# A graph network layer on one core: three-operation features on ScalarE, an earlier last adjacency load, earlier statistics

## The chip, the cores and the metric

The kernel runs on one core of a Trainium2 chip. The metric is device time in microseconds (us) of one execution; before the change the median of 3 runs was 1814.86 us (1811.27 to 1817.74).

A core has several engines, each with a queue of its own that it works through in order. TensorE (PE in the profile) multiplies matrices and writes to PSUM, which has eight banks here; PEld is its loading of weights. VectorE (DVE), ScalarE (ACT) and GpSimd (POOL) do elementwise work. SyncE (SP) only starts transfers (DMAs); ACT and POOL start some too. All DMAs of the core run on the same 16 DMA engines. Semaphores order the engines among each other.

## The reference

There are 32 graphs of 512 nodes with 256 features (x), each with a 512 x 512 adjacency of zeros and ones (adj). Cut to what matters:

```python
h = jnp.maximum(_layernorm(x, axis=-1), 0.0)
# _L0_gnn_ref(h, adj, ...), where h is called x:
xc = jnp.transpose(x, (0, 2, 1))
h = jax.nn.relu(_bn(_conv1d(xc, conv1_w, 0), ...))
h = _bn(_conv1d(h, conv2_w, 8), ...)                       # 17 taps
x_conv = jnp.transpose(jax.nn.relu(h + xc), (0, 2, 1))
s = x @ w_se.T + b_se                                      # 3 values a node
sq = jnp.sum(s * s, axis=-1)
dist = sq[:, :, None] + sq[:, None, :] - 2.0 * jnp.einsum('bnd,bmd->bnm', s, s)
A = jnp.exp(-dist) * mask                                  # mask = adj
msg = jax.nn.relu(x @ w_msg.T + b_msg)
x_nmp = jnp.einsum('bnm,bmd->bnd', A, msg)
x_in = jnp.concatenate([x_conv, x_nmp], axis=-1)
gi, gh = x_in @ w_ih.T + b_ih, x @ w_hh.T + b_hh           # gates r, z, n of a GRU
...
# out = x + (1 - z) * n + z * h
```

## The kernel before

The 32 graphs are worked in two groups of 16 (g = 0, 1), and each group in two stages, a first part and a nodes stage. A last stage makes the gates of all graphs, two graphs (a pair) at a time. All matrices are float32; a matmul appears in the profile as two halves. Within each stage the order of the instructions on every engine is the order of the program's text (`manual_schedule`), so where a line stands decides what it queues behind.

**First part** (`first_part`). For each graph b: `load_x` brings x; `statistics` takes mean and variance on VectorE (bn_stats, bn_aggr, an addition) and the inverse root on POOL (rstd); `normalise` writes xn on VectorE, or for one graph of the second group on ScalarE with a small shift from VectorE ahead of it; `transpose_h` transposes it on TensorE (phT) and clips it on VectorE into hT, which is also stored to DRAM (hd); `conv1` multiplies by w1 (pc), VectorE adds the shift (h) and ScalarE clips; `windows_to_freq` transforms windows of h into 80 frequency rows (px, into xf). In group 0 the 17-tap weights go through the same transform between these steps (pw, wst, stored as wd), and the steps of `load_weights` come one per graph.

**Nodes stage** (`nodes`). Two kinds of work are woven together. One is the convolution in frequency: 40 units a group, each a `product` of three matmuls in place of four (py), for which `prepare` forms two sums on POOL, wsum (128x512) and both (128x256); `load_unit` brings a unit's weights (wt) into one of three buffers. Its result y is stored (yd) through the list `stores`, which `flush` empties in order on SP. The other is the graph product, for the graphs in the order of `todo`. `message` multiplies by wmsg, whose last three columns are w_se: TensorE makes pm, VectorE adds the bias to msg and to the three embedding columns st, ScalarE clips msg. `features` builds from st and its square the factors fl and fr, whose product over 9 rows is the exponent -dist. `factors` transposes them on TensorE (psl, psr), `exponents` multiplies them (pd) and ScalarE takes exp into A. `turn` transposes the adjacency on VectorE, `masked` multiplies A by it. `aggregate7` forms A times msg in seven products, for which `block_sums` makes eight sums on POOL (ms, ts and two in place); the last graphs of group 1 use the plain `aggregate` (L528). `save_nmp` stores the result (nd).

The loop over i takes graph todo[i] and looks ahead: adjacency loads run two graphs ahead, into two buffers by turns, h loads four ahead, message and features two ahead, factors one ahead. At the head of an iteration stand

```python
flush()
...
if len(more) > 1:
    load_adj(more[1], i % 2)
if len(more) > 3:
    load_h(more[3])
```

`more` holds the next four graphs, so it has two left at i = 13, where the last adjacency is loaded. An adjacency is four DMAs of 256 KB. In group 1 the units end at i = 12.

In group 0 the last four units (36 to 39) are left over and are worked in the first part of group 1, in five pieces that `fill()` takes one after the other from the list `left`.

**Gate stage**. `load_pair` and `load_combined` bring the first pair's h (hp), frequencies (yt), nmp (np) and the combined weights (sw) on POOL's queue; `sums` forms POOL sums of them; `inverse` transforms back (L659, pc); the gates multiply by sw in seven products (pg, pn, pz; L671).

Of the kernel before, what the change touches and what calls it, by code (L numbers as in the profile page):

```python
# [13 lines left out]
ALU = mybir.AluOpType  # L14
# [51 lines left out]
def gnn_layer(  # L66
# [131 lines left out]
    def shift_w1():  # L198
# [3 lines left out]
    wmsg = early.tile([P, DC, D + NS], FP, name="wmsg")  # L202
    bmsg = early.tile([P, D + NS], FP, name="bmsg")

    load_weights = [
        partial(nc.sync.dma_start, back, nc.inline_tensor(back_np, name="dft_back").ap()),
        partial(load_rows, wmsg[:, :, :D], w_msgT, nc.sync),
# [2 lines left out]
        partial(nc.sync.dma_start, bmsg[:, D:], b_se.rearrange("t o -> o t").to_broadcast([P, NS])),  # L210
        load_vectors,
        vectors,
    ]


# [2 lines left out]
    fr = early.tile([P, NC, 4, 32], FP, name="fr")  # L218
    nc.vector.memset(fl, 0.0)
    nc.vector.memset(fr, 0.0)  # L220
    nc.vector.memset(fl[:, :, 2 * NS : 3 * NS], 1.0)
    nc.vector.memset(fr[:, :, :, NS : 2 * NS], -1.0)


    WD = dram.tile([ROWS, D * D + 4 * D], FP, name="wd")
# [79 lines left out]
    def transpose_h(b):  # L305
        HT[b] = work.tile([P, DC, N], FP, tag="hT", name=f"hT_{b}")
        for dc in range(DC):
            p = bank(f"phT_{b}_{dc}")
            for c in range(NC):
                nc.tensor.transpose(p[:, c * P : (c + 1) * P], XN[b][:, c, dc * P : (dc + 1) * P], ident)  # L310
            if b == 0 and dc > 0:
                nc.scalar.activation(HT[b][:, dc, :], p, AF.Relu)
            else:
                nc.vector.tensor_scalar(HT[b][:, dc, :], p, 0.0, None, op0=ALU.max)  # L314
        nc.sync.dma_start(HD[b], HT[b])
        del XN[b]
# [136 lines left out]
    def features(b):  # L453

        st = ST.pop(b)
        nc.vector.tensor_mul(st[:, 1], st[:, 0], st[:, 0])
        s1, s2 = (st[:, k, :, None, :].to_broadcast([P, NC, 4, NS]) for k in range(2))
        nc.vector.tensor_copy(fl[:, :, :NS], st[:, 0])
        nc.vector.tensor_copy(fl[:, :, NS : 2 * NS], st[:, 1])
        nc.vector.tensor_scalar(fr[:, :, :, :NS], s1, 2.0, None, op0=ALU.mult)  # L460
        nc.vector.tensor_scalar(fr[:, :, :, 2 * NS : 3 * NS], s2, -1.0, None, op0=ALU.mult)

    def factors(b):

# [421 lines left out]
    def first_part(g, freq, between, left=()):  # L886


        b0, b1 = g * GB, (g + 1) * GB
        for b in range(b0, b0 + 3):  # L890
            if b not in X and (g == 0 or b == b0):
                load_x(b)
        if g == 0:
            t = XN[b0] = pools["first"].tile([P, NC, D], FP, tag="xn", name="rows", bufs=2)
            ones, diags = t[:, 0, :P], t[:, 1:3, :].rearrange("p i (c m) -> p i c m", m=P)
            nc.vector.memset(ones, 1.0)

            for _ in range(5):
                nc.tensor.matmul(row1[1][:, : 2 * P], ident, fr.rearrange("p c g k -> p (c g k)")[:, : 2 * P], start=True, stop=True)
            batch_norm("bn1", scale1, shift1, nc.gpsimd)  # L900
            bn1_row(0, scale1, ones, diags)
            bn1_row(1, shift1, ones, diags)
        if b0 not in STATS:
            statistics(b0)
        normalise(b0)
        if g == 0:
            scale_w1()
            shift_w1()
        left = list(left)

        def fill():
            for step in left.pop(0) if left else ():
                step()

        if g > 0:
            place_h1(b0)
            load_x(b0 + 1)
            fill()
            load_x(b0 + 2)
        transpose_h(b0)  # L920
        fill()
        statistics(b0 + 1)
        normalise(b0 + 1, g > 0)
        fill()
        if g > 0:
            statistics(b0 + 2)
        for b in range(b0, b1):
            if b + 3 < b1:
                load_x(b + 3, nc.sync if b < 3 else nc.gpsimd)
            if b == b0:  # L930
                conv1(b)
                one, two = between(0) if g == 0 else ([], [])
                for step in one:
                    step()
                fill()
                if g == 0:
                    transpose_h(b + 1)
                    statistics(b + 2)
                    normalise(b + 2)
                else:  # L940
                    normalise(b + 2)
                    transpose_h(b + 1)
                fill()
                xf, last_two = freq(g), two
                continue
            if g == 0:

                slots = last_two if b == b0 + 1 else between(b - b0)

                def slot():  # L950
                    for step in slots.pop(0) if slots else ():
                        step()

                if b == b0 + 1:
                    between(b - b0)
                    conv1(b)
                    slot()
                if b == b0 + 2:
                    slot()
                if b == b1 - 1:  # L960
                    by_chunks(b - 1)
                    load_h(b0)
                if b + 2 < b1:
                    statistics(b + 2)
                if b + 1 < b1:
                    transpose_h(b + 1)
                if b > b0 + 2:
                    slot()
                if b + 2 < b1:
                    normalise(b + 2)  # L970
                if b > b0 + 1:
                    conv1(b)
                    slot()
                if b == b1 - 1:
                    by_chunks(b)
                windows_to_freq(b - 1, xf)
                slot()
                continue
            if b == b1 - 1:
                by_chunks(b - 1)  # L980
                load_h(b0)
            if b + 2 < b1:
                statistics(b + 2)
            if b + 1 < b1:
                transpose_h(b + 1)
            if b + 2 < b1:
                normalise(b + 2)
            one, two = between(b - b0)
            conv1(b)
            for step in one:  # L990
                step()
            windows_to_freq(b - 1, xf)
            for step in two:
                step()
        if g > 0:
            by_chunks(b1 - 1)
        windows_to_freq(b1 - 1, xf)
        return xf
# [8 lines left out]
    with tc.tile_pool(name="freq", bufs=1) as fpool:  # L1007
# [33 lines left out]
        def nodes(g, xf, units, last, following=()):  # L1041
# [45 lines left out]
            for i, b in enumerate(todo):  # L1087
                mine = spread(units, i, last) if i < last else []
                more = todo[i + 1 : i + 5]
                seven = i <= last  # L1090

                def bring():
                    if len(more) > 1:
                        message(more[1])
                        features(more[1])

                flush()
                if g + 1 < NG and i == GB // 2:
                    load_x(b1)
                if g + 1 < NG and i == 3 * GB // 4:  # L1100
                    statistics(b1)
                if len(more) > 1:
                    load_adj(more[1], i % 2)
                if len(more) > 3:
                    load_h(more[3])
                if more:
                    factors(more[0])
                if i == 0:
                    bring()
                for u in mine[:1]:  # L1110
                    multiply(u)
                if i > 0:
                    bring()
                if not seven:
                    aggregate(b, [0])
                if more:
                    turn(more[0], [0, 1])
                    exponents(more[0])
                    masked(more[0], [0, 1])
                for u in mine[1:2]:  # L1120
                    multiply(u)
                if more:
                    turn(more[0], [2, 3])
                    masked(more[0], [2, 3])
                if seven:
                    aggregate7(b)
                else:
                    aggregate(b, [1])
                if len(more) > 2:
                    by_chunks(more[2])  # L1130
                stores.append(partial(save_nmp, b))
                for u in mine[2:]:
                    multiply(u)
                if more and i + 1 <= last:
                    block_sums(more[0])
            flush()

        with phase("pw", "ahead"):
# [3 lines left out]
            with phase("first", "sums"):  # L1142
                combine = combine_weights()

                def between(b):

                    if b == GB - 3:
# [4 lines left out]


                pw, (u0, u1, u2, u3) = pools["pw"], range(UNITS - LEFT, UNITS)
                left = [[partial(load_unit, 0, u2, pools["sums"])],
                        [partial(prepare, pw, 0, u1, xf), partial(product, pw, 0, u0, xf), partial(prepare, pw, 0, u2, xf)],
                        [partial(product, pw, 0, u1, xf), partial(load_unit, 0, u3)],
                        [partial(prepare, pw, 0, u3, xf), partial(product, pw, 0, u2, xf)],
                        [partial(product, pw, 0, u3, xf)]]
# [82 lines left out]
```

## Time and profile before

| what | us |
|---|---|
| median of 3 runs | 1814.86 (1811.27 to 1817.74) |
| the profiled execution | 1818.6 |
| its span, first to last instruction | 1816.8 |
| TensorE, VectorE, POOL, ScalarE busy | 1791.6, 1244.6, 779.4, 623.5 |
| first part, nodes of group 0 | to about 157, to about 434 |
| first part, nodes of group 1 | to about 555, to about 851 |
| gate stage | from about 851 |
| one graph in nodes of group 0, of group 1 | 16.5, 19.1 |
| one pair in the gate stage | 59.7 |

Stage ends are where TensorE turns to the next kind of work in the timeline; the periods are the distances of equal steps of neighbouring graphs there. TensorE's granted clock is 0.996 on the mean of the span.

A timeline line gives the start in us from the span's start, the duration, the engine, the source line, the operation, output and inputs, their shapes, and how many neighbours were merged; in brackets stands the idle time just before it and who ended that. SPq, ACTq and POOLq are DMA issues of these queues. A wait line reads: who waited, for whom, us in total, times, longest. A windows line gives for one stretch the length and then the busy us of TensorE, its weight loads, VectorE, ScalarE and POOL, each with its number of instructions, then the granted clock as a share of full speed, the DMA engines' mean busy share and GB/s. "Landing" is the time from a DMA's issue to its completion.

### The profile page before, as it was taken

To read this page: it belongs to the slowest core of one execution; us is meant where nothing else is said; L and a number is where in the kernel's file an instruction comes from. 1 tells how busy PE (TensorE), PEld (TensorE's weight loads), DVE (VectorE), ACT (ScalarE), POOL (GpSimd) and SP (SyncE) were. 2 spreads that over 40 slices of the span, in tenths; PEclk is the share of its full clock that TensorE was granted. 3 is DMA by queue.
4 is the path that set the end of the run, shared out by engine and by line. 5 is a ranking of instruction groups with operands and counts; after the bars stand their busy time and mean duration, and the time that the engine had idled before them with its cause. 6 is when DMAs were issued, how large, how long until landed. Compare 5 with 4: busy or idle time off the path is not lost.

```text
span 1816.8 us, 21203 instructions
## 1 busy us (share of the span) xinstructions
PE 1791.6 (99%) x6974; PEld 1151.6 (63%) x6974; DVE 1244.6 (69%) x2370; ACT 623.5 (34%) x1252; POOL 779.4 (43%) x731
## 2 busy tenths in 40 slices
PE   9999999999999999998999999999999999999998
PEld 6677788887998888884544554455545554555443
DVE  7886988996996778783266546664666456655666
ACT  4556444443345444443212222122212221222121
POOL 3432877777334777775322232213231322133221
PEclk9999999999999999999999999999999999999999
DMA  9999889785769878979142144224432343234412
GB/s 261 305 296 226 239 231 231 220 222 191 251 222 222 243 216 221 253 188 309 23 122 87 35 122 122 87 36 121 122 98 45 101 122 110 52 82 122 118 21 53
DMA packets 307089, 288.27 MB, mean 159 GB/s; under 512 B 146764, under 2 KB 237420, under 8 KB 306596
## 3 DMA queue, kind: packets, MB, share of 16 engines
q1 hardware_dynamic: 296948, 261.44, 53.3%
q0 software_dynamic: 6592, 23.50, 4.2%
q10 hardware_dynamic: 3440, 1.97, 0.4%
q8 instruction: 56, 0.92, 0.2%
q14 instruction: 53, 0.43, 0.1%
HBM read 190.45 MB, written 96.40 MB: 158 GB/s over the span
## 4 chain that ended last, share of the span: by engine, by line
PE 90%; DMA 3%; DVE 3%; issue 2%; POOL 1%; SPq 0%; ACT 0%; ACTq 0%; DVEq 0%; POOLq 0%
PE pg L671 30%; PE pn L671 15%; PE py L394 11%; PE pn L545 9%; PE pm L445 6%; PE pc L330 5%; PE pc L659 5%; PE px L345 3%; PE pd L489 2%; PE pw L254 2%; PE phT L310 1%; DMA adj<-in_adj_dram 1%; DMA wt<-wd 1%; PE pz L671 1%; DMA x<-in_x_dram 1%
## 5 line engine op out<-in xcount | busy, mean ns | idle before, releaser
L649 POOL TENSOR_TENSOR hp<-hp 128x512 f32<-128x512 f32 x64 | 80.4, 1267 | 415.9 <-DMA hp<-hd 325.7
L671 PE MATMUL pg<-hp,sw 128*128 128x512 f32 x434 | 221.8, 593 | 0.7 <-DVE rz L690 0.5
L671 PE MATMUL pg<-np,sw 128*128 128x512 f32 x434 | 221.6, 592 | 0.0
L671 PE MATMUL pg<-cp,sw 128*128 128x512 f32 x434 | 221.6, 592 | 0.0
L649 POOL TENSOR_TENSOR cp<-cp 128x512 f32<-128x512 f32 x64 | 80.5, 1268 | 235.6 <-ACT cp L665 234.3
L361 POOL TENSOR_TENSOR wsum<-wt 128x512 f32<-128x512 f32 x78 | 105.6, 1354 | 121.7 <-DMA wt<-wd 76.9
L686 ACT ACTIVATE rz<-rz,brz 128x512 f32<-128x512 f32 x93 | 67.0, 721 | 260.2 <-DVE rz L690 260.2
L394 PE MATMUL py<-wt,xf 128*128 128x256 f32 x640 | 154.3, 384 | 0.0
L671 PEld LDWEIGHTS pg<-hp,sw 128*128 128x128 f32 x434 | 82.2, 190 | 104.7 <-issue 98.1
L671 PEld LDWEIGHTS pg<-cp,sw 128*128 128x128 f32 x434 | 82.5, 190 | 103.8 <-issue 103.8
L671 PEld LDWEIGHTS pg<-np,sw 128*128 128x128 f32 x434 | 82.5, 190 | 103.8 <-issue 103.8
L394 PEld LDWEIGHTS py<-wt,xf 128*128 128x128 f32 x640 | 117.1, 190 | 35.0 <-issue 19.7
L810 ACT ACTIVATE nt<-nt,vech 128x512 f32<-128x512 f32 x64 | 46.2, 722 | 236.2 <-DVE nt L809 236.2
L330 PE MATMUL pc<-w,hT 128*128 128x256 f32 x512 | 118.3, 384 | 0.8 <-DVE hT L314 0.8
L445 PE MATMUL pm<-wmsg,hq 128*128 128x259 f32 x512 | 117.8, 382 | 0.3 <-DVE nmp L563 0.3
L671 PE MATMUL pn<-np,sw 128*128 128x512 f32 x224 | 114.4, 592 | 0.0
L671 PE MATMUL pn<-cp,sw 128*128 128x512 f32 x224 | 114.4, 592 | 0.0
L671 PE MATMUL pn<-hp,sw 128*128 128x512 f32 x224 | 114.4, 592 | 0.0
L495 DVE TENSOR_TENSOR A<-A,at 128x512 f32<-128x512 f32 x128 | 111.2, 906 | 0.0
L330 PEld LDWEIGHTS pc<-w,hT 128*128 128x128 f32 x512 | 95.4, 191 | 23.8 <-issue 5.6
L445 PEld LDWEIGHTS pm<-wmsg,hq 128*128 128x128 f32 x512 | 96.4, 189 | 15.6 <-DVE nmp L563 0.7
L659 PEld LDWEIGHTS pc<-back,yt 128*128 128x128 f32 x640 | 92.7, 190 | 7.7 <-issue 7.7
(173 smaller groups left out, 3429.2 us busy)
## 6 DMA issues: line engine op xcount, KB each, us to landing
wt<-wd SPq DMA_DIRECT2D x80, 512.0 KB, 7.6
adj<-in_adj_dram SPq DMA_DIRECT2D x128, 256.0 KB, 6.6
wd<-wst SPq DMA_DIRECT2D x64, 320.0 KB, 5.9
yd<-y SPq DMA_DIRECT2D x76, 256.0 KB, 5.1
yt<-yd SPq DMA_DIRECT2D x30, 640.0 KB, 6.8
hd<-hT SPq DMA_DIRECT2D x32, 512.0 KB, 4.6
nd<-nmp SPq DMA_DIRECT2D x32, 512.0 KB, 3.0
xb<-in_x_dram SPq DMA_DIRECT2D x128, 128.0 KB, 3.7
```

Of the source, the lines that this page charges most:

```text
L330: nc.tensor.matmul(p[:, j, :], HT[b][:, ic, c * P : (c + 1) * P], w1[:, ic, :], start=(ic == 0), stop=(ic == DC - 1))
L345: nc.tensor.matmul(p[:, j * 2 * L : (j + 1) * 2 * L], H1[b][:, c0 + j, ic * P : (ic + 1) * P], fwd, start=True, stop=True)
L361: nc.gpsimd.tensor_tensor(t, WT[g, u][:, 0], WT[g, u][:, 1], op=ALU.add)
L394: nc.tensor.matmul(dst, v[:, ic, :], w[:, ic, :], start=(ic == 0), stop=(ic == DC - 1))
L445: nc.tensor.matmul(p[:, : D + NS], hq[:, ic, c * P : (c + 1) * P], wmsg[:, ic, :], start=(ic == 0), stop=(ic == DC - 1))
L495: nc.vector.tensor_mul(A[b][:, mc, :], A[b][:, mc, :], AT.pop((b, mc)))
L545: nc.tensor.matmul(bk, left[:, k, :], right[:, k, :], start=(first and k == 0), stop=(k == 1), skip_group_check=True)
L649: nc.gpsimd.tensor_tensor(t[:, dst, :], t[:, a, :], t[:, b, :], op=sub)
L659: nc.tensor.matmul(bk[:, t0:t1], YT[p][j][:, c, oc * P : (oc + 1) * P], back[:, n : n + t1 - t0], start=(c == 0), stop=(c == len(spans) - ...
L671: nc.tensor.matmul(bk[:, t], sw[:, k, q, o, :], terms[k][q][:, t], start=(first and i == 0), stop=(i == len(ks) - 1), skip_group_check=True)
L686: nc.scalar.activation(rz[:, g, j, :], src, AF.Sigmoid, bias=brz[:, g : g + 1], scale=1.0)
L810: nc.scalar.activation(n, n, AF.Tanh, bias=b_in[:, i : i + 1], scale=1.0)
```

## The change

It has four parts.

1. `features` no longer scales. The embedding's weights and bias are multiplied once by the root of two, on POOL, by a new last step of `load_weights` (`scale_embedding`), and the constants in fl and fr become -0.5, so that the same exponent results from unscaled copies of st and its square. In place of four VectorE operations there are three copies on ScalarE: one for both parts of fl, and one for each of two parts of fr. The square stays on VectorE.
2. In `nodes` the last adjacency (two graphs left) is loaded ahead of `flush()`; the other loads of an iteration stand in a new function `ahead`. For i > 0 it is called where they stood.
3. For i = 0 `ahead` is called after the first unit's `multiply`, which issues the next unit's weight load, so that this goes ahead of one adjacency and one h load.
4. In the first part of group 1 `statistics` of the second and third graph move ahead of a `fill()` each, and the first left-over `prepare` moves from the second piece of `left` to the first. With the left-over work in these places, the second graph's statistics stand ahead of product 36's sums, and the third graph's ahead of product 37's. For group 0 there is nothing in `left`, so this part changes nothing there.

On TensorE the instructions and their order stay the same. On VectorE, apart from the four features operations of each graph, only the order at the start of group 1's first part changes. On POOL two operations are added, and one rstd changes place with the wsum and both of unit 38. On SP nothing is added: in each nodes stage one weight load changes place with an adjacency and an h load, and the last adjacency passes a y store and an nd store in group 0, and one y store in group 1.

```diff
+    def scale_embedding():
+
+        for t in (wmsg[:, :, D:], bmsg[:, D:]):
+            nc.gpsimd.tensor_scalar(t, t, float(np.sqrt(2.0)), None, op0=ALU.mult)
+
     load_weights = [
...
         vectors,
+        scale_embedding,
     ]
...
-    nc.vector.memset(fl[:, :, 2 * NS : 3 * NS], 1.0)
-    nc.vector.memset(fr[:, :, :, NS : 2 * NS], -1.0)
+    nc.vector.memset(fl[:, :, 2 * NS : 3 * NS], -0.5)
+    nc.vector.memset(fr[:, :, :, NS : 2 * NS], -0.5)
...
         nc.vector.tensor_mul(st[:, 1], st[:, 0], st[:, 0])
-        s1, s2 = (st[:, k, :, None, :].to_broadcast([P, NC, 4, NS]) for k in range(2))
-        nc.vector.tensor_copy(fl[:, :, :NS], st[:, 0])
-        nc.vector.tensor_copy(fl[:, :, NS : 2 * NS], st[:, 1])
-        nc.vector.tensor_scalar(fr[:, :, :, :NS], s1, 2.0, None, op0=ALU.mult)
-        nc.vector.tensor_scalar(fr[:, :, :, 2 * NS : 3 * NS], s2, -1.0, None, op0=ALU.mult)
+        nc.scalar.copy(fl[:, :, : 2 * NS].rearrange("p c (k n) -> p k c n", n=NS), st)
+        for k, at in enumerate((0, 2 * NS)):
+            nc.scalar.copy(fr[:, :, :, at : at + NS], st[:, k, :, None, :].to_broadcast([P, NC, 4, NS]))
...
         transpose_h(b0)
+        statistics(b0 + 1)
         fill()
-        statistics(b0 + 1)
         normalise(b0 + 1, g > 0)
-        fill()
         if g > 0:
             statistics(b0 + 2)
+        fill()
...
+                def ahead():
+                    if len(more) > 2:
+                        load_adj(more[1], i % 2)
+                    if len(more) > 3:
+                        load_h(more[3])
+
+                if len(more) == 2:
+                    load_adj(more[1], i % 2)
                 flush()
...
-                if len(more) > 1:
-                    load_adj(more[1], i % 2)
-                if len(more) > 3:
-                    load_h(more[3])
+                if i > 0:
+                    ahead()
                 if more:
                     factors(more[0])
                 if i == 0:
                     bring()
                 for u in mine[:1]:
                     multiply(u)
+                if i == 0:
+                    ahead()
...
-                left = [[partial(load_unit, 0, u2, pools["sums"])],
-                        [partial(prepare, pw, 0, u1, xf), partial(product, pw, 0, u0, xf), partial(prepare, pw, 0, u2, xf)],
+                left = [[partial(load_unit, 0, u2, pools["sums"]), partial(prepare, pw, 0, u1, xf)],
+                        [partial(product, pw, 0, u0, xf), partial(prepare, pw, 0, u2, xf)],
```

## The prediction

> **What bounds the kernel now.** I read the busy table first, then the list of what TensorE waited for, then the timelines around the three longest of those waits.
>
> ```profile
> PE 1791.6 (99%) x6974; PEld 1151.6 (63%) x6974; DVE 1244.6 (69%) x2370; ACT 623.5 (34%) x1252; POOL 779.4 (43%) x731
> ```
>
> TensorE is busy 99% of the span, and the changed program issues the same matmuls in the same order. Faster helpers alone are therefore worth nothing; a change can only win where TensorE stands still. The list of its waits (total us, times, longest) names those places:
>
> ```profile
> PE pn L528 <- DVE A L495: 7.0, 1, 7.0
> PE py L394 <- POOL both L374: 4.0, 1, 4.0
> ...
> PE pn L545 <- POOL ts L520: 1.1, 1, 1.1
> ```
>
> *First place, end of the second nodes stage.* Timelines of SP, VectorE and TensorE, then two slices of the windows view (its last columns: granted clock, DMA share, GB/s):
>
> ```profile
> 815.21 0.32 SPq L568 DMA_DIRECT2D nd<-nmp  x1
> 815.84 1.00 SPq L1057 DMA_DIRECT2D yd<-y  x2
> 816.89 2.68 SPq L414 DMA_DIRECT2D adj<-in_adj_dram  x4
> ```
>
> ```profile
> 838.96 1.30 DVE L478 STREAM_TRANSPOSE at<-adj 128x512 f32<-128x512 f32 x2 [12.48 <-DMA adj<-in_adj_dram]
> ```
>
> ```profile
> 841.74 9.71 PE L528 MATMUL pn<-A,msg 128*128 128x512 f32 x16 [7.04 <-DVE A L495]
> 851.29 5.81 PE L659 MATMUL pc<-back,yt 128*128 128x136 f32 x40
> ```
>
> ```profile
> 812.00:814.00 2.00, 2.00 (x11) 1.77 (x10) 1.97 (x2) 0.41 (x2) 1.92 (x2) 1.00 0.00 0
> 844.00:846.00 2.00, 2.00 (x3) 0.50 (x2) 1.75 (x3) 0.00 (x0) 0.49 (x1) 0.50 1.02 417
> ```
>
> The last graph's adjacency is issued at 816.9, behind two stores, and lands 19.8 us after its last piece was issued, because POOL's first loads of the gate stage start at 818.2 and share the DMA engines. VectorE waits for it until 839, TensorE until 841.7, and then runs at clock 0.50. At 812 to 814 the DMA engines had been idle.
>
> *Second place, start of the second first part.* Timelines of TensorE and POOL:
>
> ```profile
> 453.46 1.21 PE L394 MATMUL py<-wsum,both 128*128 128x256 f32 x4 [3.98 <-POOL both L374]
> 454.46 1.91 PE L310 MATMUL phT<-ident,xn 128*128 128x128 f32 x8
> 456.16 4.43 PE L330 MATMUL pc<-w,hT 128*128 128x256 f32 x16
> ```
>
> ```profile
> 449.64 1.01 POOL L289 TENSOR_TENSOR rstd<-rstd,minus_half 128x4 f32<-128x4 f32 x1 [5.50 <-DVE rstd L288]
> 450.60 0.83 POOL L118 DMA_DIRECT2D x<-in_x_dram  x1
> 451.45 1.28 POOL L361 TENSOR_TENSOR wsum<-wt 128x512 f32<-128x512 f32 x1
> 452.67 0.74 POOL L374 TENSOR_TENSOR both<-xf 128x256 f32<-128x256 f32 x1
> ```
>
> POOL is idle 5.5 us in front of an rstd whose statistics are late on VectorE; the last left-over product's two sums stand behind it and reach TensorE 4 us late.
>
> *Features on VectorE*, in the timeline just ahead of the first place:
>
> ```profile
> 800.71 0.77 DVE L458 COPY fl<-st 128x12 f32<-128x12 f32 x1
> 801.39 1.32 DVE L459 COPY fl<-st 128x12 f32<-128x12 f32 x1
> 802.62 1.32 DVE L460 TENSOR_SCALAR fr<-st 128x48 f32<-128x48 f32 x1
> 803.87 0.78 DVE L461 TENSOR_SCALAR fr<-st 128x48 f32<-128x48 f32 x1
> ```
>
> Four copies of 12 to 48 elements hold VectorE for 3.8 us here; the shortest such copy took 0.16.
>
> **What the Trainium skill says.** "SBUF — State Buffer", SBUF: two separate sides: VectorE and GpSimd share a port pair as an exclusive lock, held for a whole instruction. The trace agrees: the small copies take 0.16 us with POOL idle and up to 1.32 beside a 1.27 us POOL sum. ScalarE has its own ports. "ScalarE: Activation LUTs", What ACT_TABLE_LOAD costs: an activation with immediate scale takes 186 ns + 0.833 ns per element, and neighbours overlap by 93; for 24 and 48 elements that gives my estimate of 0.21 and 0.23 us, some 0.4 for the three. No such copy is in the trace; the nearest row is the 128x128 one at 0.266. "TensorE: Matmul & The Clock Gate", What's actually happening: about 3.4 us of idleness halve TensorE's clock. The trace agrees: 0.50 after 7.0 us, 0.55 to 0.60 after 4.0. "DMA: Bandwidth & Descriptors", Queues, rings and completion order: a DMA engine takes packets from its queues in turn. This fits the four adjacency pieces, landing in 5.1 us at best and 19.8 at worst while POOL's queue was filling.
>
> **The change part by part.**
>
> *Features (32 times).* Off VectorE: four operations, 13.2 + 23.5 + 18.9 + 22.7 = 78 us in the groups. Onto ScalarE: three, about 0.4 us, behind the message's second Relu and ahead of the four exponentials. The copies wait for VectorE's square of st, so exponentials slip 0.4 to 1.0 us. Queued behind them are the y copies of a product, then aggregate7's copies, whose first waits for TensorE anyway (0.99 us idle at 765.8). VectorE masks later than the exponentials but loses its own features first, so masks come about 1.5 us sooner, not later. In the steady loop this is worth nothing. It costs in the opening, where nothing lies between features and factors: at 563.66 TensorE transposed fl just as fr was done; now Relu ends at 563.85 and the copies near 564.2, so psr is 0.4 us late. At 166.0 the same. The first graph of each stage has 0.6 us of cover. Cost +0.6 for both stages (0 if a bank wait at 172 absorbs one, 2 if each handshake is dearer).
>
> *Root two.* Two POOL operations on 6 and 3 elements, once, at some 90 us, where POOL is three tenths busy: nothing; without that cover, 2 us at POOL's 1.0 us for an rstd.
>
> *Last adjacency.* In the second stage only one of the two stores moves behind its four DMAs: the other y store and an nd store stay ahead. By itself that is worth 0.5 us of issue. But the nd store waited until 815.2 for VectorE's sums, and the other for its y sums behind them. With 3.8 us taken off VectorE at 800 to 805, and exponentials at about 801.5 to 803.5, I get y sums of product 37 at 804.3, masks finished by 807.5 to 808.5, nmp by 810, product 38's y at 812.4 (TensorE finishes it at 811.7). So the adjacency is issued at about 812.9 to 815.5, into idle DMA engines; with landings of 5.8 to 8.2 us as one matrix earlier it is there by 819 to 823. POOL's loads come at about 817. VectorE is free at 826.5 and the exponentials end at 833.2, so anything before about 830 is early enough. TensorE then goes from 834.5 on at 0.44 us per 512-wide half product: 16 take 7.0, and pc starts at 841.5 instead of 851.3. Gain 9.7. Bounds: 2 if only the 0.5 us is realised, 10 at most. Next late would be the second part of sw, issued by POOL at 836.9 to 838.5 with landings up to 12.8 us, so by 851; Q2 needs it four groups of 2.57 us after 847, at 857. In the first nodes stage the four DMAs pass a y store and an nd store; TensorE waits for no adjacency there: 0.
>
> *Opening order (i = 0).* One weight load goes ahead of five DMAs (four adjacency, one h). In the first stage it was issued at 178.9 behind them and POOL waited 7.0 us for it until 187, so ts was late by the 1.1 us in the list. Now it is free to go when product 0 is done, near 172, and lands near 180. Gain 1.1. The five DMAs slip 2 us against a use at 191 or later; the next weight load slips 1 to 2 us. Second stage: nothing.
>
> *Statistics before sums.* VectorE is free at 436.6, x of the next graph is there by 438.7, so its statistics end at 440.5 as before; the u0 sums move behind them, and nobody waits for those. POOL does that rstd before sum u2 (weights land at 441.2 either way). The second statistics wait for their x: the two landings must be about 5 and 6 to 7 us, so it arrives near 443; rstd on POOL at 446.3, load x, wsum and both of u3 ready at 449.1. TensorE needs them at 449.3: the 4 us go. Late next is VectorE: y(u2), four xn, two hT end at 452.3, so conv1 starts at 452.5 instead of 456.2, at full clock (3.45 us instead of 4.3): px at 456.0 instead of 460.4. Gain 4.4, from 1 (x lands late) to 6 (VectorE no limit).
>
> *Sum.* -9.7 - 4.4 - 1.1 + 0.6 = **-14.6 us**. The profiled execution took 1818.6 (span 1816.8), which becomes 1804.0; it was 3.7 above the runs' median of 1814.9, so I forecast a median of **1800.3**.
>
> **Rivals.**
> 1. The adjacency still collides with POOL's loads: it stays behind a y store, and if VectorE is not relieved there it leaves only 0.5 us sooner. For: both loads move with VectorE. Against: idle DMA at 812. Gain 3 instead of 9.7: 1807.
> 2. The left-over stall changes its owner: the second statistics wait for x in VectorE's queue and hold h, xn and hT. For: landing near 443 is inferred. Gain 1: 1803.7.
> 3. Slower: ScalarE becomes the late engine. Features put ahead of the exponentials delay masks, POOL's block sums and so aggregate7, in every graph. At 0.7 us for 30 graphs, +21: 1821. It decides from the point where masks slip by more than the gap to POOL's first use of them: 2.3 us in the first stage (mask ends 390.5, POOL's sum starts 392.8), 5.8 in the second. A slip of 1 us against VectorE's relief speaks against it.
> 4. The gate stage starts 10 us sooner but its weights or pair 1's loads, now sharing the DMA engines, are late, and give back 6: 1806.
>
> **How the numbers follow.** Forecast 0.64 (own range 1796 to 1804, its costs' bounds with some 3 us of spread between runs); rival 1: 0.14; rival 2: 0.10; rival 4: 0.08; rival 3: 0.04. A third of rival 1 and half of rival 4, joined by another loss, stay within 0.3% (5.4 us, about what a measurement here can tell from no change): same 0.09, slower 0.04, faster 0.87. Range 1795 to 1808: the forecast's own, rival 2, and most of rivals 1 and 4.
>
> **What would show it.** Right: no wait of L528 for A; TensorE's clock 1.00 through 835 to 850; pc of the gate stage some 15 us earlier; the last adjacency issued at least 3 us before POOL's first hp load; no wait of py for both near 449; steady matrix periods unchanged at 19.1 us. Wrong: a new wait for fl or fr of over 1 us, longer periods in a nodes stage, or a wait for sw or hp behind the inverse.

## The result, and the profile after

The changed kernel takes 1805.48 us (median of 4 runs, 1805.07 to 1809.2) against 1814.3 for the kernel before (4 runs, 1811.27 to 1817.74): ratio 0.9955, 95% interval 0.9933 to 0.9978. A second set gave 1805.31 against 1814.67, ratio 0.9955 (0.9943 to 0.9967). The profiled execution took 1805.07, with a span of 1803.0. The forecast was 1800.3, with a range of 1795 to 1808: direction and range held, but the gain is 9 us and not 14.6, and the median lies outside the 1796 to 1804 that the prediction gave its own mechanism. The ratios, here and below, come from the runs themselves and differ a little from the quotients of the medians.

The busy table of the page after, and then its list of TensorE's waits (total us, times, longest):

```profile
PE 1787.2 (99%) x6974; PEld 1149.2 (64%) x6974; DVE 1215.6 (67%) x2242; ACT 636.7 (35%) x1348; POOL 792.8 (44%) x733
```

```profile
PE pn L532 <- DVE A L499: 2.1, 2, 1.6
PE row L903 <- DVE fr L228: 1.9, 1, 1.9
PE phT L316 <- DVE xn L308: 0.9, 1, 0.9
PE pc L336 <- DVE hT L320: 0.8, 2, 0.5
PE psl L470 <- ACT fl L463: 0.5, 2, 0.3
```

Source lines have moved by 4 to 6 (L528 is now L532, L394 is L400, L545 is L549). The 4.0 us wait of py for both and the 1.1 us wait for ts are gone. The wait for A fell from 7.0 to 2.1 and has not gone. VectorE did 29 us less and ScalarE 13 more.

This table of stage starts on TensorE is read from the timelines. "Before, again" is a second profile of the unchanged kernel, from the first experiment.

| TensorE reaches (us) | before | before, again | after |
|---|---|---|---|
| nodes of group 0 | 157.3 | 156.0 | 156.7 |
| first conv1 (pc) of the second first part | 440.6 | 444.3 | 438.4 |
| its first px | 460.4 | 465.0 | 452.6 |
| nodes of group 1 | 554.9 | 559.5 | 548.0 |
| last psl (features turned) | 825.9 | 830.5 | 819.4 |
| pc of the gate stage | 851.3 | 850.2 | 837.5 |

From the first profile to the profile after, pc of the gate stage came 13.8 us sooner: 2.2 of them ahead of the second first part, 4.7 from there to the nodes of group 1 (114.3 became 109.6), 7.3 between the last psl and pc (25.4 became 18.1), less 0.4 in the nodes of group 1. The second profile of the unchanged kernel tells another story: there pc follows the last psl after 19.7 us, and 3.7 us more than in the first profile are lost by the second first part. From the first pg of the gate stage to the last product it is 951.6 us before and after.

The place of the last adjacency in the timeline after (SP and POOL, then VectorE and TensorE; the number in brackets is the idle time before the instruction and who ended it):

```profile
805.13 0.32 SPq L572 DMA_DIRECT2D nd<-nmp  x1
805.99 0.32 SPq L1061 DMA_DIRECT2D yd<-y  x1
806.36 2.43 SPq L420 DMA_DIRECT2D adj<-in_adj_dram  x4
808.89 0.77 SPq L1061 DMA_DIRECT2D yd<-y  x1
...
819.92 1.30 DVE L482 STREAM_TRANSPOSE at<-adj 128x512 f32<-128x512 f32 x2
...
823.69 5.99 POOL L653 TENSOR_TENSOR hp<-hp 128x512 f32<-128x512 f32 x4
...
825.30 3.23 DVE L499 TENSOR_TENSOR A<-A,at 128x512 f32<-128x512 f32 x2 [4.09 <-ACT A L495]
...
833.14 4.56 PE L532 MATMUL pn<-A,msg 128*128 128x512 f32 x10 [1.63 <-DVE A L499]
```

POOL's first hp load follows at 810.7, so the adjacency leads by 4.3 us and has long landed when VectorE transposes it at 819.9. Now VectorE waits 4.09 us for exponentials, and its first two masks take 3.23 us beside POOL's four sums, where two took 1.25 at 816.5 with POOL idle.

The start of the second first part, after:

```profile
444.04 1.30 POOL L367 TENSOR_TENSOR wsum<-wt 128x512 f32<-128x512 f32 x1
445.28 0.74 POOL L380 TENSOR_TENSOR both<-xf 128x256 f32<-128x256 f32 x1
...
447.03 1.03 PE L400 MATMUL py<-wsum,both 128*128 128x256 f32 x4
447.89 1.16 PE L316 MATMUL phT<-ident,xn 128*128 128x128 f32 x8
448.98 3.79 PE L336 MATMUL pc<-w,hT 128*128 128x256 f32 x16
452.61 2.34 PE L351 MATMUL px<-fwd,h 128*128 128x160 f32 x16
```

POOL has the last left-over sums ready at 446.0 instead of 453.4, TensorE no longer stops at py, and px comes 14.2 us after the first pc instead of 19.8.

### The profile page after: what moved, and what is told of

Its sections match the earlier page's. It is cut to its first block, busy times and chain, and to the rows that moved or that the text cites. A ratio compares the mean times of both kernels' runs of the same rounds, so it can differ in the third digit from the quotient of the medians.

```text
span 1803.0 us, 21211 instructions
## 1 busy us (share of the span) xinstructions
PE 1787.2 (99%) x6974; PEld 1149.2 (64%) x6974; DVE 1215.6 (67%) x2242; ACT 636.7 (35%) x1348; POOL 792.8 (44%) x733
## 4 chain that ended last, share of the span: by engine, by line
PE 95%; DVE 2%; issue 1%; POOL 1%; ACT 0%; DMA 0%; ACTq 0%; DVEq 0%; POOLq 0%
PE pg L675 30%; PE pn L675 15%; PE py L400 12%; PE pn L549 10%; PE pm L451 6%; PE pc L336 6%; PE pc L663 5%; PE px L351 4%; PE pd L493 2%; PE pw L260 2%; PE phT L316 1%; PE pz L675 1%; PE psr L475 1%; PE pn L532 0%; DVE xn L308 0%
## 5 line engine op out<-in xcount | busy, mean ns | idle before, releaser
L367 POOL TENSOR_TENSOR wsum<-wt 128x512 f32<-128x512 f32 x78 | 113.4, 1454 | 101.3 <-DMA wt<-wd 59.7
L400 PE MATMUL py<-wt,xf 128*128 128x256 f32 x640 | 154.2, 384 | 0.0
L499 DVE TENSOR_TENSOR A<-A,at 128x512 f32<-128x512 f32 x128 | 137.4, 1112 | 5.4 <-ACT A L495 5.3
L400 PEld LDWEIGHTS py<-wt,xf 128*128 128x128 f32 x640 | 117.1, 190 | 34.9 <-issue 19.0
```

The costliest lines, as they stand in the source:

```text
L367: nc.gpsimd.tensor_tensor(t, WT[g, u][:, 0], WT[g, u][:, 1], op=ALU.add)
L400: nc.tensor.matmul(dst, v[:, ic, :], w[:, ic, :], start=(ic == 0), stop=(ic == DC - 1))
L499: nc.vector.tensor_mul(A[b][:, mc, :], A[b][:, mc, :], AT.pop((b, mc)))
```

## The experiments

All times are medians; ratios are to the kernel before, run beside them on the same chip. There it took 1815.98 (52 runs) beside the first four kernels, 1814.67 (24 runs) beside the next four (part 3 alone, part 4 alone, the earlier exponentials and the changed kernel again), and 1815.63 (15 runs) beside the last four, which undo or delay a part in the changed kernel. The three groups ran on three chips, so a difference between kernels of two groups can hold a difference between chips. One execution of each kernel was profiled; with the first profiles of the two kernels that makes 14, and where a part's worth is read from the length of a stage, all of them are compared.

### Was the adjacency's stall the kernel's, or that one execution's?

The unchanged kernel once more, and the last adjacency's move (part 2) as the only edit of it:

```diff
+                if len(more) == 2:
+                    load_adj(more[1], i % 2)
                 flush()
...
-                if len(more) > 1:
+                if len(more) > 2:
                     load_adj(more[1], i % 2)
```

> The kernel before, unchanged, profiled a second time. Theory S (the size of the adjacency stall varies between executions, and the first profiled one, 4 us above the median, had a long one): the points where TensorE starts a stage agree with the first profile to 0.5 us up to 826, and the stretch from there to the gate stage's first matmul (24.9 us in the first profile) differs by 2 us or more. Theory E (the profiled execution was slow elsewhere): that stretch is again within 1 us of 24.9, and another stage is shorter. Ratio to before 1.000 in both.

Measured: 1815.78 (14 runs), ratio 0.9992 (0.9978 to 1.0006). In its profile the 7.0 us wait is not there. The waits of the unchanged kernel, second profile:

```profile
PE pn L528 <- DVE A L495: 2.1, 2, 1.6
...
PE pd L489 <- DVE nmp L563: 1.0, 1, 1.0
```

It took 1817.5, only 1 us less than the first profile's 1818.6: it loses time elsewhere. So neither theory held whole: the stretch behind the last psl did shrink, from 25.4 to 19.7 us, but the stages ahead of it differ by far more than 0.5 us (table above). The features and opening experiments show where.

> Only the last adjacency ahead of flush. Own theory (two parts needed): it passes one store and is issued 0.5 to 1 us sooner, because the nd store ahead of it still waits for VectorE's late sums; the L528 wait stays at 4 us or more: 0 to -3 us. Rival O (the order alone does it): the adjacency leads POOL's hp load by over 3 us, the wait falls below 2.5 us, and the time is 7 us lower.

Measured: 1816.15 (14 runs), ratio 0.9993 (0.9982 to 1.0004); wait for A 2.0. Rival O's signs came, a lead of 3.2 us and a short wait, but not its 7 us: the kernel beside it mostly has no such stall to lose. The move alone is worth nothing that a median shows.

The opposite edit is the changed kernel with only its last adjacency put back behind the stores:

```diff
-                if len(more) == 2:
-                    load_adj(more[1], i % 2)
                 flush()
+                if len(more) == 2:
+                    load_adj(more[1], i % 2)
```

> The changed kernel with its last adjacency behind the stores again, as before; all else as changed. Its issue should fall from 3 to 4 us ahead of POOL's first hp load to about 1 us ahead of it, a smaller lead than the 1.3 us of the one profile in which it landed 19.8 us late. Theory A (that landing is rare, not set by the lead; in four of five profiles with this order TensorE waited only 1.2 to 2.1 us): time within 1 us of the changed kernel, wait of pn for A 2 us. Theory B (the forecast: a lead of this size collides with POOL's loads): 6 to 10 us longer than the changed kernel, wait of pn for A 6 us or more.

Measured: 1806.11 (6 runs, 1805.27 to 1809.5), ratio 0.9939 (0.9917 to 0.9961); wait for A 2.1. These are theory A's signs: no collision.

To price one, the same kernel loads that adjacency twice behind the stores, which also adds 1 MB of traffic:

```diff
-        for g in range(4):
+        for g in list(range(4)) * times:
             nc.sync.dma_start(ADJ[b][32 * g : 32 * (g + 1)], rows[g])
...
                 flush()
+                if len(more) == 2:
+                    load_adj(more[1], i % 2, 2)
```

> The changed kernel with the last adjacency behind the stores and loaded twice into the same tile, so that its second four DMAs (256 KB each, extra traffic) start beside or after POOL's first loads of the gate stage. It prices a forced collision. If the forecast's mechanism is right as a mechanism: the second load lands 12 to 20 us after its issue, TensorE waits 5 to 12 us for A and runs at half clock after it, 6 to 14 us longer than the changed kernel. Rival: the queues share the DMA engines without such a delay, the second load lands in 5 to 8 us, time within 2 us of the changed kernel.

Measured: 1827.42 (6 runs), ratio 1.0053 (1.0032 to 1.0073), 22 us above the changed kernel's median on the other chip and beyond both expectations. The wait for A is 16.8 us. Not all of it is this collision: from the last psl to pc its profile has 34.2 us instead of 18.1, 16.0 more; the first group loads its last adjacency twice too, and some 4 us more are lost there, between its last psl and the second first part. The view of the tile adj in the window around 804 to 836 gives the first and last issue of its DMAs on SP and their landings; first before, then the kernel with it put back, then the late one:

```profile
L414 SPq DMA_DIRECT2D adj<-in_adj_dram x4: 487/656/739, 816.9 to 819.1; - x4
...
DMA to landing us min/median/max: 5.1/13.8/19.8
```

```profile
L420 SPq DMA_DIRECT2D adj<-in_adj_dram x4: 424/490/548, 811.8 to 813.4; - x4
...
DMA to landing us min/median/max: 4.8/5.7/8.1
```

```profile
L420 SPq DMA_DIRECT2D adj<-in_adj_dram x8: 311/456/2527, 813.3 to 823.1; - x8
...
DMA to landing us min/median/max: 3.8/8.1/24.2
```

POOL's first hp load was issued at 818.2, 813.3 and 814.7. So the last piece went out 0.9 us after it (landing up to 19.8), 0.1 after it (8.1), and 8.4 after it (24.2; each piece of the second load is issued only when the same piece of the first has landed). In the four other profiles with the adjacency behind the stores it went out 0.0 to 2.6 us before it and landed within 7.9. This fits what the prediction took from "DMA: Bandwidth & Descriptors", Queues, rings and completion order, as a mechanism: a piece that is behind POOL's loads shares the engines with them. But the distance alone does not set the landing: a piece 0.2 us behind POOL's first load took 13.8 us before (issued at 818.4) and one as far behind took 8.1 in the late kernel (at 814.9). A late landing is in one of the six profiles with that order; what else decides it, and how often it comes in runs without a profile, stays open.

### What are the features worth?

> Features on ScalarE and the root two alone. Own theory (two parts needed): the y store still stands ahead of the last adjacency and POOL's loads move forward with VectorE, so the adjacency starts at most 2 us before POOL's first hp load and still waits: 0 to -3 us against before, with +0.6 us in the two openings. Rival R (relief of VectorE alone does it): the L528 wait for A falls below 2.5 us and the time is 7 us lower. Rival C (ScalarE is late): +5 us or more, with longer periods in the nodes stages.

The edit is part 1 of the diff above alone. Measured: 1813.31 (15 runs), 2.7 below the kernel before on that chip, ratio 0.998 (0.997 to 0.9991). With part 2 added:

> Both parts together, without the other two. Own theory: they act together, so the gain exceeds the sum of the two alone: -4 to -8 us against before, the adjacency leads POOL's hp load by some 4 us, and what stays of the wait is the masks' own (about 2 us). Rival: gains add up, and one of the two alone already has nearly all of it.

Measured: 1814.37 (22 runs), ratio 0.9987 (0.9978 to 0.9996): again nothing for the adjacency, and not the 4 to 8 us that were expected of the two together. And the changed kernel with part 1 undone:

> The changed kernel with the four features operations on VectorE again. Theory (from the features alone, 2.7 us below the kernel before, and from matrix periods of 17.1 to 20.1 us in the first nodes stage that occur only with features on VectorE): 2.5 to 4 us longer than the changed kernel, a spread of its times of more than 5 us instead of about 5, and one or more periods of the first nodes stage above 16.6 or 19.2 us. As forecast on record: features cost TensorE nothing in the steady loop and gain 0.6 in the openings, so within 0.6 us of the changed kernel, or 0.6 us faster.

Measured: 1808.84 (10 runs), ratio 0.9955 (0.9937 to 0.9974). The runs go from 1804.73 to 1815.52; the changed kernel's, from 1805.07 to 1809.86 in both sets. The best executions are equal. The median is 3.4 us above the changed kernel's on another chip, and 1.7 to 2.7 above the two kernels run with it that keep the features on ScalarE (1807.19 and 1806.11). By ratio to the kernel before, the intervals overlap (0.9955 is the changed kernel's ratio too), so the times of this kernel alone settle nothing. The profiles do: TensorE waits for VectorE here. Its waits:

```profile
PE pm L445 <- DVE nmp L563: 0.9, 1, 0.9
...
PE pd L489 <- DVE nmp L563: 0.5, 1, 0.5
```

How such a stall comes about is seen in VectorE's and TensorE's timeline of the unchanged kernel's second profile:

```profile
406.60 2.83 DVE L495 TENSOR_TENSOR A<-A,at 128x512 f32<-128x512 f32 x2
409.35 0.94 DVE L559 TENSOR_TENSOR nmp<-nmp,p 128x256 f32<-128x256 f32 x1
410.22 0.95 DVE L560 TENSOR_TENSOR nmp<-nmp,p 128x256 f32<-128x256 f32 x1
411.20 1.37 DVE L561 TENSOR_TENSOR nmp<-nmp 128x256 f32<-128x256 f32 x1
...
412.50 0.41 DVE L563 TENSOR_TENSOR nmp<-nmp,pn 128x256 f32<-128x256 f32 x1
412.96 1.13 PE L489 MATMUL pd<-sr,sl 9*128 9x512 f32 x4 [0.97 <-DVE nmp L563]
414.02 3.65 PE L394 MATMUL py<-wt,xf 128*128 128x256 f32 x8
```

and in three slices of its windows view and of that of the kernel with the features alone (busy us of TensorE, its weight loads, VectorE, ScalarE, POOL; granted clock, DMA share, GB/s):

```profile
408.00:412.00 4.00, 3.99 (x20) 2.57 (x17) 3.97 (x5) 1.45 (x4) 3.92 (x4) 1.00 0.08 32
412.00:416.00 4.00, 3.04 (x9) 1.93 (x10) 4.00 (x8) 2.17 (x4) 3.92 (x5) 0.75 0.44 139
```

```profile
412.00:416.00 4.00, 4.00 (x21) 3.51 (x20) 4.00 (x7) 2.02 (x7) 4.00 (x4) 1.00 0.64 194
```

The nmp sums (L559 to L565) add up the pieces of the graph product. Two masks take 2.83 us and three of these sums 0.94 to 1.37 while POOL is busy all the time; the same sums take 0.42 with POOL idle, and the fourth, which has one input in PSUM (pn), takes 0.41 beside POOL too. That fits the exclusive lock of "SBUF — State Buffer", SBUF: two separate sides. VectorE is full (3.97 of 4.00), TensorE waits, and for 4 us its mean clock is 0.75. The list gives this stall 1.0 us, but the eight py halves behind it take 3.65 us, where the kernel with the features alone has 1.99; the graph's next pn starts 10.7 us behind psl instead of 7.0.

A full slice is not the cause by itself: with the features on ScalarE VectorE is as full from 412 to 416 (4.00 of 4.00), and TensorE does not wait. What differs is how early VectorE is. At the last psl of the first nodes stage, the sum that TensorE waited for (L563, now L567) starts 2.2 to 4.9 us after that psl in the six profiles with the features on VectorE, and from 0.3 us before to 0.6 after it in the eight with them on ScalarE. The distances from psl to psl in the first nodes stage show it as well: from the fourth to the fifteenth they are 16.5 or 19.1 us throughout in all eight profiles with the features on ScalarE. In each of the six with the features on VectorE at least one is longer, by 0.2 to 1.1 us. From the fourth psl to the first pc of the second first part those six take 240.3 to 244.5 us, and seven of the eight take 239.2 to 239.4 (the eighth is the double load): 3.2 us less on the mean. The second nodes stage gives back 0.6 up to its last psl (270.8 us on the mean of the six, 271.4 with the features on ScalarE). What makes VectorE later in one execution than in another was not followed up.

### The statistics, the opening, and one step further

Part 4 alone on the kernel before:

> The kernel before with the statistics-before-sums part alone (both edits of it, the order in the first part and the list of left-over work). Theory (this part is worth more than forecast, since in the changed kernel conv1's last accumulation to the next stage's start went from about 20 to 14.2 us): 5 to 7 us below the kernel before, no wait of py for both in the list of TensorE's waits, conv1 to px 14 to 15.5 us. As forecast on record: 4.4 below, with VectorE's hT late (py wait gone, pc at full clock). Rival 2 of the prediction (the second statistics hold VectorE waiting for x): at most 1 below, with a wait of phT or pc for VectorE of about 3 us in its place.

Measured: 1810.03 (11 runs) against 1814.67, ratio 0.9975 (0.9966 to 0.9985): 4.6 us. The wait of py for both is gone, first pc to px 14.4 us. By the median the forecast's 4.4 is nearer than the theory's 5 to 7; by the stage it is not. From the first pc of the second first part to the nodes of group 1 the eight profiles with this part take 108.8 to 110.2 us and the six without it 114.2 to 115.7: 5.6 less on the mean. Rival 2 falls.

Part 3 alone, and the changed kernel with part 3 undone (the call of `ahead` back in its old place for i = 0):

> The kernel before with the opening part alone: at i = 0 the adjacency and h loads come after the first weight load. Theory, as forecast: 1.1 us below the kernel before, the 1.1 us wait of pn for ts gone, that weight load issued near 172 instead of 178.9. Rival: the five DMAs behind it make the next adjacency late and the gain is nothing (0 to 0.3 below), with a wait for A or msg near 190 to 215.

> The changed kernel with the loads of i = 0 ahead of the first multiply again, as before; all else as changed. As forecast on record: 1.1 us longer than the changed kernel, with the wait of pn for ts of about 1.1 us near 196 back. Rival: no difference (within 0.4 us), since with the features off VectorE the nodes stage has other slack.

Measured: alone 1816.56 (14 runs), ratio 1.0007 (0.9992 to 1.0022), no gain shown; undone in the changed kernel 1807.19 (6 runs), ratio 0.9946 (0.9925 to 0.9967), 1.9 above the changed kernel's median beside the other set. The times do not settle it; the traces do. The weight load went out at 171.8 with part 3 alone and at 171.9 after, against 178.9 before, and TensorE did not wait there. Undone, TensorE's timeline has

```profile
196.04 1.13 PE L549 MATMUL pn<-ts,ms 128*128 128x256 f32 x4 [1.24 <-POOL ts L524]
```

and it reaches the next psl at 200.5 instead of 199.1. From the first psl of the first nodes stage to the fourth, the seven profiles with this part take 36.7 to 37.3 us and the seven without it 37.7 to 39.7: 1.8 less on the mean, more than the 1.1 us of the wait.

The wait for A that is left, 2.1 us, had two suspects: exponentials that start late, and POOL's sums that stretch the masks. The changed kernel was run with the last graph's exponentials a step earlier, and once more as it is:

```diff
-                if more:
+                if more and (i < GB - 2 or i <= last - 1):
                     factors(more[0])
...
+                if not seven and i == GB - 2 and not more[1:]:
+                    exponents(more[0])
                 if not seven:
                     aggregate(b, [0])
...
-                    exponents(more[0])
+                    if seven or i < GB - 2:
+                        exponents(more[0])
...
+                if len(more) == 2 and i + 1 > last:
+                    factors(more[1])
```

> The changed kernel with the last graph's factors put ahead of the last but one graph's eighth aggregate and its exponentials at the head of the last but one step, to see whether the 2.1 us for which TensorE still waits for the last A come from exponentials that start late (theory), or from POOL's hp sums that stretch VectorE's two masks from 1.3 to 3.3 us each (rival). Theory: wait of pn for A below 0.5 us, inverse up to 2 to 3.5 us sooner after the last psl, 2 to 3.5 us below the changed kernel. Rival: the wait stays at 1.5 to 2.1 us, time within 0.7 us of the changed kernel.

> The changed kernel itself, unchanged, for more executions and a second profile. If the parts add up (features 2.5 to 3, first part 5 to 7, opening 1, last adjacency about 0 in the median): 8.5 to 11 us below the kernel before. If the last adjacency's 9.7 us were a property of the kernel before and not of its one profiled execution: 14 or more below. Profile: pn waits 1.6 to 2.2 us for A, as in its first profile; inverse 17.5 to 20 us after the last psl.

Measured: 1802.41 (5 runs, 1801.37 to 1804.2), ratio 0.9934 (0.9922 to 0.9946), against 1805.31 and 0.9955 (0.9943 to 0.9967) for the changed kernel run with it. The timeline of the earlier exponentials:

```profile
820.68 14.00 PE L532 MATMUL pn<-A,msg 128*128 128x512 f32 x32
820.83 2.06 ACT L495 ACTIVATE A<-pd 128x512 f32<-128x512 f32 x4 [2.46 <-PE pd L493]
...
823.89 3.45 DVE L499 TENSOR_TENSOR A<-A,at 128x512 f32<-128x512 f32 x2
```

The last two masks are stretched as before (3.45 us), and TensorE runs its 32 half products in one piece. So earlier exponentials are enough to remove the wait, and the stretching does no harm where VectorE is early. It is part of the wait all the same: in the profile of part 4 alone the exponentials start as late, but the first two masks take 2.36 us instead of 3.23, and TensorE waits 1.2 us instead of 2.1. Masks at 1.25 us for two would, by an estimate from the lines after, have ended near 829, ahead of TensorE's need at 830; that was not tried. This version beats both kernels.

## Why the prediction was right, and where it was not

- **Last adjacency: the step that failed.** "TensorE goes from 834.5 on ... pc starts at 841.5 instead of 851.3. Gain 9.7", and then carrying the whole sum over to the median. The stall was in one of six profiles with that order. The likely value for the median was about 0 (ratio 0.9993 alone; 0.7 us when put back, on another chip). The profile of before had given a sign: its execution was 3.7 us above the median. Even against that execution the term was too large, 7.3 instead of 9.7: with the adjacency early, TensorE still waits 2.1 us for A. The prediction let TensorE run on at 834.5, 1.3 us behind the end of the exponentials; in fact four masks stand between, and beside POOL's sums they take 3.2 to 3.4 us for two, not 1.25.
- **Features: mis-sized.** "In the steady loop this is worth nothing" holds for an execution in which VectorE is never late, and the lowest times agree. For the median it was worth 2.7 us alone; by the stages it is 3.2 gained between the first nodes stage and the first part behind it, and 0.6 lost in the second nodes stage. The prediction read the stretched copies (3.8 us for four) and did not ask how close VectorE was to being late in other graphs. Its 78 us off VectorE count operations that overlap: VectorE's busy time fell by 29 us between the two first profiles, and by 38 from the second one of the kernel before to the features alone. Its cost in the openings was right in size: +0.6 forecast, and the waits of psl for fl come to 0.5 after. The copies run about 0.22 and 0.24 us each, against the estimate of 0.21 and 0.23 from "ScalarE: Activation LUTs", What ACT_TABLE_LOAD costs, and the three together 0.5, not 0.4.
- **Statistics: right in size.** 4.4 forecast, from 1 to 6; 4.6 alone by the median, 4.7 between the two profiles, 5.6 by the stage in all of them. Its next late piece was wrong: VectorE's hT was to hold conv1 until 452.5, and it began at 449.0; 0.9 of the gain was given back on the way to the nodes stage.
- **Opening: right in place.** The load and the wait are as forecast in the trace, and the stage gains 1.8 us, not 1.1; the time of the part alone shows no gain.
- **Rivals.** The times of rivals 4 (1806), 1 (1807) and 2 (1803.7) all lie nearer than the forecast's, but not for their reasons: the gate stage takes the same time; the adjacency does not collide after, and did in one of six profiles of the old order; no stall changed its owner at the left-over sums. Rival 3 did not come: the periods stay at 16.5 and 19.1 us.
- **The sum.** By medians, the parts alone come to -2.7 + 0.2 + 1.9 - 4.6 = -5.2, and the whole to -9.4. Most of that gap comes from adding medians of times that spread unevenly: the means of the same runs give -3.7 - 0.6 + 1.6 - 5.3 = -8.0, and -8.7 for the whole. By the stages of the 14 profiles it is -2.6 - 1.8 - 5.6 = -10.0, with nothing for the adjacency. So the parts about add up, and no help of one part for another is needed or shown. That the total landed in the range is luck in part: an adjacency term that was too large by about 9 met a features term that was too small by about 3 and two terms that were too small by about 1 each.

## What to carry to other kernels

A stall that shows in one profile is a property of that execution until a second one shows it, and a profiled execution that lies above the median of the runs is a hint that most do not have it. Before an edit is priced at nothing because its engine is not the bound, ask how early its results are ready for the engine that is the bound: where that lead is small, a delay elsewhere becomes a wait. The spread of the times and the length of one stage in many profiles tell more than the best time. After a stall is cut, follow the next input in the same queue (here the exponentials) back to the step that issues it; it may be had for a few lines.

## What the runs showed of the hardware that was not expected

- 256 KB pieces of the last adjacency land in 3.8 to 8.1 us when issued ahead of POOL's burst of loads or, in two profiles, 0.1 and 0.2 us behind its start, but in a third one issued 0.2 us behind took 13.8, and four that were 0.9 to 8.4 us behind took 15.1 to 24.2.
- After waits of only 2.0 to 2.3 us, in two pieces within 4 us, ten half products took TensorE 4.56 us in six profiles and 6.1 to 6.3 in four. After a single wait of 0.97 us its clock was 0.50 from 414.0 to 416.6. "TensorE: Matmul & The Clock Gate", What's actually happening, speaks of about 3.4 us of idleness; here shorter waits were enough, and the outcome at about 2 us was not the same from run to run.
- Masks with two inputs in SBUF take 1.25 us for two, and 2.3 to 3.5 beside POOL's sums, which themselves go from 5.2 to 6.0 us for four.
